# A two-layer graph attention kernel: products of layer 1 ahead of the next block's sums, its blocks in another order, and another beginning of layer 0

## The chip, the cores and the metric

The kernel runs on one core of one Trainium2 chip. The metric is the device time of one execution in microseconds (us). The core has five engines with queues of their own: TensorE (PE in the profile; its weight loads are PEld), VectorE (DVE), ScalarE (ACT), GpSimd (POOL) and SyncE (SP), and 16 DMA engines that they feed.

## What is computed

Two layers of graph attention over 2708 nodes of 1024 features, with a residual and a layer norm after each. The adjacency matrix has about 16 ones in a row.

```python
def layer0(x, adj):                       # Wf, bf, Wg, bg, W, bW
    f = x @ Wf + bf
    g = x @ Wg + bg
    e = relu(f @ g.T)
    attention = softmax(where(adj > 0, e, NEG), axis=1)
    return attention @ (x @ W + bW)

def layer1(x, adj):                       # W, a1, a2
    h = x @ W
    e = leaky_relu(h @ a1 + (h @ a2).T, 0.2)
    attention = softmax(where(adj > 0, e, NEG), axis=1)
    return relu(attention @ h)

x = layernorm(x + layer0(x, adj))
x = layernorm(x + layer1(x, adj))
```

## The kernel before

**Lists instead of a matrix.** A first stage (to about 220 us) reads the adjacency matrix, makes a list of neighbours of each node, sorts the nodes by the length of their lists and deals them out. It also multiplies `Wf` and `Wg` into one matrix `M`. After that both layers work on lists. A path for other inputs (`general_path`) is not run here.

**Blocks, groups and tiles.** The nodes stand in 22 blocks: block 0 has 20 nodes, the other 21 have 128 each, in four groups of 32. The neighbours of a group are fetched in tiles: one tile is one indirect DMA, issued by GpSimd, that brings 128 rows of 1024 numbers (four neighbours of each of 32 nodes), 0.5 MB. How many tiles a block needs is fixed by the constants `SORTED` and `BLOCKS` (lines 40 to 58): 3 for block 0, 15 for blocks 1 and 21, 16 for blocks 19 and 20, and 20 for each of the others, 405 in all. Both layers fetch all 405. Layer 0 fetches rows of `x` into a ring of 20 slots; layer 1 fetches rows of the table `T1`, which layer 0 wrote, into 32 slots (`ring` and `more`). `Layer.gathers` (line 656) issues the next gathers in order, each as soon as the tile that held its slot has been used. `SL` holds the lists, `SL0` a copy for the first tiles with its indices clamped.

**A block's work in layer 1** (lines 988 to 1110):

- `scores1` (line 1009): VectorE takes a score from a column of each tile, then `Layer.soft` (line 663) makes the weights: maxima, an exponential on ScalarE, the weights spread into matrices `st`, and row sums `rs`.
- `Layer.sums` (line 693): TensorE first adds `rs` over a group's four parts (`pt`), then adds up the tiles with their weights in the PSUM tile `po`; four groups run side by side. Each tile that is done frees its slot. ScalarE then scales `po` into `y` by the reciprocals.
- `turn` (line 517): TensorE transposes `y` into `pt` tiles, ScalarE copies them to `yT`.
- `product` (line 535): `yT` times `W1` (in the buffer `M`) in a PSUM tile `pm`: 32 matmuls in the trace. Block 0, with only 20 nodes, uses `split_product` (line 558): the eight pieces of the sum run side by side in four parts of the array, ScalarE copies the parts out, and a second product with `rep` adds them up in all four places.
- `close1` (line 1027): the residual comes by a DMA from `X1S` on SP's queue, VectorE adds and normalises (`norm`, line 594), ScalarE applies it to `z`, and GpSimd scatters `z` to the output.

Layer 0 is built in the same way, with more: the product of `x` and `M` comes first (`f_product`, line 796), is copied by ScalarE so that each group of 32 rows stands four times (`Fr`), and is multiplied by each tile on VectorE (`dots`, line 812). After the sums comes the product with `Wt` (`W`). `close` (line 828) also writes `X1S` and scatters to `T1`.

**What sets the order.** The engines' work is wrapped in `InOrder` (line 61): each engine runs its instructions strictly in the order in which the program issues them. So the order of the lines is the schedule, and an instruction that waits holds all that follow it on its engine. In layer 1 before the change, the loop over blocks (lines 1068 to 1101) issues for block k: the sums of k; the product of block k-1 (lines 1081 to 1085); the transposes of k; the closing of block k-2; the scores of k+1. The copies from `pt` to `yT` of block k follow at the start of the next round (lines 1074 to 1076). The product of k-1 thus stands between the sums of k and the transposes of k. The blocks are taken in the order 0 to 21 (line 996).

**Layer 0's beginning** (lines 858 to 906) takes block 1 first, then block 0, then 2 and on. It issues: the product of block 1 in two `pm` tiles (line 877), the copies of it to `Fr` (lines 884 to 891), q of block 2 (line 892), the product of block 0 with its copy to `Fr` (`f_small`, lines 799 to 804), the transposes of block 2 with their copies (`x_turn`, line 894), the load of block 3 and lists of 4, the product of block 2 (line 897), the load of `W` into `Wt` from ScalarE's queue (line 900), the dots of block 1 and its softmax (lines 901 to 904). Two `pm` tiles, two `pt` tiles and one `po` tile exist.

Of the kernel before, what the change touches and what calls it, by code (L numbers as in the profile page):

```python
# [8 lines left out]
F32 = mybir.dt.float32  # L9
# [3 lines left out]
ALU = mybir.AluOpType  # L13
# [93 lines left out]
def listed_path(ctx, tc, x, adj, Wf, bf, Wg, bg, W, bW, W1, a1, a2, out):  # L107

    nc = tc.nc
    P = 128  # L110
# [13 lines left out]
    Q = 4  # L124
# [430 lines left out]
            half_product(halves[h], h, n, xT, w, row)  # L555
        return halves

    def split_product(xT, w, parts, row=None):

        pm = ps_m.tile([P, H, 512], F32, name="pm")
        for h in range(H):
            c = slice(h * 512, (h + 1) * 512)
            if row is not None:
                pe.matmul(pm[:32, h, :], ones3[row:row + 3, :32], rows3[row:row + 3, c], start=True, stop=False)
            for k in range(KC // Q):
                for p in range(Q):
                    i = p * KC // Q + k
                    pe.matmul(pm[32 * p:32 * p + 32, h, :], xT[:, i, :32], w[:, i, c],  # L570
                              start=(k == 0 and (row is None or p > 0)), stop=(k + 1 == KC // Q))
        act.copy(parts, flat(pm))
        yield
        pm = ps_m.tile([P, H, 512], F32, name="pm")
        for h in range(H):
            pe.matmul(pm[:, h, :], rep, parts[:, h * 512:(h + 1) * 512], start=True, stop=True)
        return pm

    def whole(steps):

# [42 lines left out]
    def cut(most, turns, order):  # L623


        units, at = [], 0
        for i, b in enumerate(order):
            u = Unit()
            u.b, u.gs, u.at = b, groups[b], at
            u.G, u.T, u.n = len(u.gs), max(TILES[g] for g in u.gs), nrows[b]  # L630
            u.tiles = [(k, g, t) for k, g in enumerate(u.gs) for t in range(TILES[g])]
            u.col = {(k, t): m for m, (k, g, t) in enumerate(u.tiles)}
            u.tiles.sort(key=lambda m: (m[0] // turns, m[2]))
            u.sc = scores[i % 2][:, :u.G, :u.T]
            assert len(u.tiles) <= min(most, MOST)
            at += len(u.tiles)
            units.append(u)
        return units

    class Layer:  # L640
# [2 lines left out]

        def __init__(self, units, rings, width, table, stp):
            self.units, self.table, self.width, self.stp = units, table, width, stp
            self.slots = [(t, i) for t in rings for i in range(t.shape[1])]
            self.count = len(self.slots)
            self.order = [(u, g, t) for u in units for _, g, t in u.tiles]
            assert self.count <= sum(TILES[:NSL0])
            self.next, self.free, self.most = 0, set(), len(self.order)  # L650

        def rows(self, m):
# [3 lines left out]
        def gathers(self):  # L656
            while self.next < min(self.most, len(self.order)) and (self.next < self.count or self.next - self.count in self.free):
                u, g, t = self.order[self.next]
                idx = SL[:, g, t:t + 1] if self.next >= self.count else SL0[:, g, t:t + 1]
                gather(pool, self.rows(self.next), self.table, idx)  # L660
                self.next += 1

# [95 lines left out]
    with ExitStack() as s0s:  # L758
# [37 lines left out]
        def f_product(b):  # L796
            F[b] = product(nrows[b], xTs.pop(b), M, 0)

        def f_small():


            pm = whole(split_product(xTs.pop(0), M, yp.tile([P, D], F32, name="y"), 0))
            Fr[0, 0] = zs[:, :D]
            act.copy(Fr[0, 0], flat(pm))

        def replicate(b, k):

            Fr[b, k] = frp.tile([P, D], F32, name="Fr")
# [43 lines left out]

        def first_gathers(g0, g1):

            dve.tensor_scalar(SL0[:, g0:g1], SL[:, g0:g1, :], float(N - 1), None, op0=ALU.min)
            lay.gathers()

        load_x(1)
# [22 lines left out]
        for steps in (spread1, spread0):  # L881
            for _ in steps:
                pass
        for k in range(Q):
            Fr[1, k] = frp.tile([P, D], F32, name="Fr")
        for ks in ((0, 1), (2, 3)):
            for h in range(H):
                c = slice(h * 512, (h + 1) * 512)
                for k in ks:
                    for p in range(Q):  # L890
                        act.copy(Fr[1, k][32 * p:32 * p + 32, c], halves[h][32 * k:32 * k + 32, h, :])
        q_dot(2)
        f_small()
        x_turn(2)
        load_x(3)
        load_lists(4)
        f_product(2)
        spread2 = q_spread(2)
        next(spread2)
        act.dma_start(Wt, W.rearrange("(k p) d -> p k d", p=P))  # L900
        dots(units[0], 0, len(units[0].tiles))
        lay.most = len(lay.order)
        first_gathers(5, NSL0)
        soft(units[0])
        for _ in spread2:
            pass
# [81 lines left out]
    with ExitStack() as s1s:  # L988
# [4 lines left out]
        x1 = [rb, u1b]  # L993
        z1 = [u2b, zp.tile([P, D], F32, name="z1")]
        more = new_pool("ring1", 1).tile([P, R1 - R0, TW], F32, name="more")
        units = cut(R1, Q, range(NB))
        lay = Layer(units, [ring, more], TW, T1[:, :], stp)
        prod, yTs, y = {}, {}, {}


        fq = ovp.tile([P, NB, Q], F32, name="fq")
# [22 lines left out]
            dve.tensor_add(u.sc, u.sc, masked(u))  # L1024
            lay.soft(u)

        def close1(b):
            m, xt, z = valid[b], x1[b % 2], z1[b % 2]
            sp.dma_start(xt[:m], X1S[start[b]:start[b] + m, :])
            pm = prod.pop(b)  # L1030
# [5 lines left out]
            if b + 1 < NB:  # L1036
                dve.scalar_tensor_tensor(z[:m], flat(pm)[:m], 0.0, xt[:m], op0=ALU.max, op1=ALU.add)
            for _ in norm(z, m, None if b + 1 < NB else add):
                pass
            yield  # L1040
            scatter(out, ids[:m, b:b + 1], z[:m])
# [22 lines left out]
        pool.memset(over, 0.0)  # L1064
        scores1(units[0])
        closing = iter(())
        waiting = []
        for k, u in enumerate(units):
            nxt = units[k + 1] if k + 1 < len(units) else None
            b = u.b  # L1070
            back = b - 1 if b > 0 else None
            po = ps_s.tile([P, H, 512], F32, name="po")
            y[b] = yp.tile([P, D], F32, name="y1")
            if back is not None:
                for _ in yTs[back][1]:
                    pass
            if k == NB // 2 + 1:
                count_over()
            lay.sums(u, po, {6: [lambda s=closing: [None for _ in s]]}, y[b])
            closing = iter(())  # L1080
            if back is not None:
                if back > 0:
                    prod[back] = product(P, yTs.pop(back)[0], M)
                else:
                    prod[back] = whole(split_product(yTs.pop(back)[0], M, z1[1]))
            yT = tp.tile([P, KC, P], F32, name="yT")
            steps = turn(y.pop(b), nrows[b], yT, halves=True)
# [24 lines left out]

@with_exitstack
# [361 lines left out]
```

## Time and profile before

| | us |
|---|---|
| median of 3 runs | 1781.02 (1780.73 to 1785.28) |
| the profiled execution | 1778.93 |
| its span, first to last instruction | 1777.1 |
| busy: PE | 1573.1 (89%) |
| busy: DVE | 1171.4 (66%) |
| busy: ACT | 636.4 (36%) |
| busy: POOL | 1182.5 (67%) |
| layer 0, from block 1's product to the last scatter to T1 | about 228 to 1157 |
| layer 1, from its first gather to the end | 1157.4 to 1777.1 |

Times inside the execution are us from the first instruction. A line of a timeline gives the start, the duration, the engine, the operation, what it writes and reads (by the program's names), how many such instructions were merged, and in brackets how long the engine stood idle before it and what it waited for. Nearly all instructions have line 71, since one helper issues them; the names of the tiles tell them apart. In layer 1 `M` holds `W1`; in layer 0 it holds the product of `Wf` and `Wg`. The matmuls are pipelined, so that the end of one and the start of the next can overlap by some tenths.

### The profile page before, as it was taken

How to read it: one execution, taken by the hardware profiler on the slowest of the kernel's cores; microseconds unless marked ns; L12 is line 12 of the kernel's file. 1: busy time of each engine (PE TensorE's matmuls, PEld its weight loads, DVE VectorE, ACT ScalarE, POOL GpSimd, SP SyncE). 2: the span in 40 equal slices, each digit the busy share in tenths (PEclk: the TensorE clock that was granted, in tenths of full speed). 3: DMA queues.
4: the chain of work that ended last, by engine and by line, in shares of the span. 5: the costliest groups of instructions: out<-in, count | busy, mean ns of one | idle time of the engine just before them, and what ended most of it. 6: DMA issues, size and time to landing. Idle time of an engine off the chain costs nothing. (4 is left out here: it accounts for less than half of the span.)

```text
span 1777.1 us, 22911 instructions
## 1 busy us (share of the span) xinstructions
PE 1573.1 (89%) x7313; PEld 667.6 (38%) x7313; DVE 1171.4 (66%) x3539; ACT 636.4 (36%) x861; POOL 1182.5 (67%) x1191
## 2 busy tenths in 40 slices
PE   4999479899999999999999999637989988989996
PEld 2444234344444444444444444213333333333342
DVE  5879855888888888988888887513342433424442
ACT  4544454444444455555555544101111111111111
POOL 7878476467666666666666663177777777777740
PEclk9999779999999999999999999959989999999998
DMA  7646168568777777777777777299999999999960
GB/s 283 237 169 238 40 233 301 208 224 296 282 285 274 264 250 255 280 284 287 279 291 283 268 281 281 103 358 346 363 386 392 392 364 394 384 392 388 366 259 37
DMA packets 149982, 501.86 MB, mean 282 GB/s; under 512 B 32565, under 2 KB 32597, under 8 KB 147144
## 3 DMA queue, kind: packets, MB, share of 16 engines
q0 software_dynamic: 132032, 427.36, 64.8%
q1 hardware_dynamic: 10202, 55.72, 8.3%
q10 hardware_dynamic: 7618, 17.23, 2.7%
q8 instruction: 59, 0.97, 0.2%
q14 instruction: 71, 0.58, 0.1%
HBM read 509.64 MB, written 33.75 MB: 306 GB/s over the span
## 5 line engine op out<-in xcount | busy, mean ns | idle before, releaser
L71 POOL DMA_INDIRECT ring<-in_x_dram,SL x405 | 432.0, 1067 | 256.2 <-issue 89.0
L71 DVE SCALAR_TENSOR_TENSOR j<-ring,Fr 128x1024 bf16<-128x1024 f32 x402 | 494.9, 1231 | 77.0 <-DMA ring<-in_x_dram,SL 49.8
L71 ACT COPY Fr<-pm 32x1024 f32<-32x1024 f32 (+2 forms) x353 | 340.5, 965 | 20.0 <-PE pm L71 15.3
L71 PE MATMUL po<-ring,st 128*32 128x512 f32 x2660 | 338.6, 614 | 0.1
L71 POOL DMA_INDIRECT ring<-T,SL x260 | 259.6, 998 | 83.8 <-issue 58.0
L71 PE MATMUL pm<-M,xT 128*128 128x512 f32 (+1 forms) x704 | 309.7, 617 | 0.4 <-ACT xT L71 0.4
L71 PE MATMUL pm<-Wt,xT 128*128 128x512 f32 (+1 forms) x704 | 303.5, 599 | 0.0
L71 PE MATMUL pm<-M,yT 128*128 128x512 f32 (+1 forms) x704 | 298.5, 595 | 0.3 <-ACT yT L71 0.3
L71 ACT ACTIVATE scores<-scores 128x24 f32<-128x24 f32 (+5 forms) x44 | 9.8, 222 | 640.7 <-DVE scores L71 640.7
L71 PEld LDWEIGHTS pm<-M,yT 128*128 128x128 f32 (+1 forms) x704 | 127.2, 186 | 170.2 <-issue 169.7
L71 PEld LDWEIGHTS pm<-M,xT 128*128 128x128 f32 (+1 forms) x704 | 127.0, 190 | 170.6 <-issue 169.9
L71 PEld LDWEIGHTS pm<-Wt,xT 128*128 128x128 f32 (+1 forms) x704 | 125.0, 186 | 151.8 <-issue 151.4
L71 POOL DMA_INDIRECT more<-T,SL x145 | 144.1, 994 | 44.0 <-issue 32.8
L71 PEld LDWEIGHTS po<-ring,st 128*32 128x32 f32 x2660 | 102.5, 114 | 183.9 <-issue 180.0
L71 DVE TENSOR_SCALAR scores<-ring,f1q 128x2 f32<-128x2 f32 (+5 forms) x98 | 21.8, 245 | 211.3 <-DMA ring<-T,SL 209.6
L409 POOL TENSOR_TENSOR adj<-adj,iota 128x2708 f32<-128x2708 f32 (+3 forms) x23 | 130.5, 5684 | 24.9 <-ACT adj L71 24.8
L71 ACT ACTIVATE y<-po,ri 128x512 f32<-128x512 f32 (+1 forms) x88 | 55.8, 683 | 232.5 <-PE po L71 214.6
L412 DVE MAX8 cand<-adj 128x8 f32<-128x136 f32 (+2 forms) x440 | 97.2, 284 | 37.4 <-POOL adj L409 37.4
L71 PE MATMUL pm<-halfT,WfT 128*128 128x512 f32 x256 | 113.9, 600 | 1.1 <-ACT WfT L71 1.1
L71 POOL DMA_INDIRECT SL<-LD,idq x85 | 85.5, 1006 | 25.8 <-issue 20.9
L71 PE MATMUL pt<-rs,stack 128*32 128x1 f32 x680 | 14.1, 179 | 98.0 <-DVE rs L71 53.4
L71 PE MATMUL po<-more,st 128*32 128x512 f32 x580 | 94.2, 651 | 0.0
(198 smaller groups left out, 1416.9 us busy)
## 6 DMA issues: line engine op xcount, KB each, us to landing
adj<-in_adj_dram SPq DMA_DIRECT2D x21, 1354.0 KB, 5.8
X1S<-z SPq DMA_DIRECT2D x20, 512.0 KB, 6.4
ring<-in_x_dram,SL POOLq DMA_INDIRECT x405, 6.2
u1b<-X1S SPq DMA_DIRECT2D x11, 512.0 KB
rb<-X1S SPq DMA_DIRECT2D x10, 512.0 KB, 7.3
ring<-T,SL POOLq DMA_INDIRECT x260, 7.3
rows<-in_L_gnn_Wg_dram ACTq DMA_DIRECT2D x8, 512.0 KB, 4.5
rows<-in_L_gnn_Wf_dram ACTq DMA_DIRECT2D x8, 512.0 KB, 3.6
```

Of the source, the lines that this page charges most:

```text
L71: made = self.tc.keep_in_program_order(op(*args, **kwargs))
L409: nc.gpsimd.tensor_tensor(k[:n, cut], k[:n, cut], iota[:n, cut], op=ALU.mult)
L412: nc.vector.max(cand[:n, s, :], k[:n, s * SEG:min((s + 1) * SEG, N)])
```

## The change

In layer 1 the transposes of a block, their copies and its product now follow its own sums directly, ahead of the scores and sums of the next block; its closing is issued one round after its sums instead of two. The blocks are taken in the order of their tiles, fewest first: 0, 1, 21, 19, 20, 2, 3, ... 18. The buffers that alternate by block now alternate by the place in that order, and `SL0` is filled anew for the blocks whose tiles come first.

In layer 0's beginning the transposes of block 2 and the first part of block 0's product are issued right behind block 1's product. The latter goes to a `po` tile instead of a `pm` tile. The copies of block 2's transposes stand in the middle of those to `Fr` of block 1; the copy of block 0's parts stands behind them; block 0's second product and its copy to `Fr` come after block 2's product, ahead of the load of `Wt`.

```diff
-    def split_product(xT, w, parts, row=None):
+    def split_product(xT, w, parts, row=None, pm=None):
-        pm = ps_m.tile([P, H, 512], F32, name="pm")
+        pm = ps_m.tile([P, H, 512], F32, name="pm") if pm is None else pm
         for h in range(H):
...
+        yield
         act.copy(parts, flat(pm))
         yield
         pm = ps_m.tile([P, H, 512], F32, name="pm")
...
         def __init__(self, units, rings, width, table, stp):
...
+            self.first = {g: i for i, g in enumerate(g for u in units for g in u.gs)}
...
-                idx = SL[:, g, t:t + 1] if self.next >= self.count else SL0[:, g, t:t + 1]
+                idx = SL[:, g, t:t + 1] if self.next >= self.count else SL0[:, self.first[g], t:t + 1]
...
-        def f_small():
-            pm = whole(split_product(xTs.pop(0), M, yp.tile([P, D], F32, name="y"), 0))
-            Fr[0, 0] = zs[:, :D]
-            act.copy(Fr[0, 0], flat(pm))
...
+        xTs[2] = tp.tile([P, KC, P], F32, name="xT")
+        turn2 = turn(xb[2], nrows[2], xTs[2])
+        next(turn2)
+        small_f = split_product(xTs.pop(0), M, yp.tile([P, D], F32, name="y"), 0,
+                                ps_s.tile([P, H, 512], F32, name="po"))
+        next(small_f)
         for k in range(Q):
             Fr[1, k] = frp.tile([P, D], F32, name="Fr")
         for ks in ((0, 1), (2, 3)):
...
                         act.copy(Fr[1, k][32 * p:32 * p + 32, c], halves[h][32 * k:32 * k + 32, h, :])
+            for _ in turn2:
+                pass
+        next(small_f)
         q_dot(2)
-        f_small()
-        x_turn(2)
         load_x(3)
         load_lists(4)
         f_product(2)
         spread2 = q_spread(2)
         next(spread2)
+        Fr[0, 0] = zs[:, :D]
+        act.copy(Fr[0, 0], flat(whole(small_f)))
         act.dma_start(Wt, W.rearrange("(k p) d -> p k d", p=P))
         dots(units[0], 0, len(units[0].tiles))
...
-        units = cut(R1, Q, range(NB))
+        order1 = sorted(range(NB), key=lambda b: (sum(TILES[g] for g in groups[b]), b))
+        units = cut(R1, Q, order1)
         lay = Layer(units, [ring, more], TW, T1[:, :], stp)
-        prod, yTs, y = {}, {}, {}
+        done1 = {b: i for i, b in enumerate(order1)}
+        for u in units:
+            g, at = u.gs[0], lay.first[u.gs[0]]
+            if u.at < lay.count:
+                dve.tensor_scalar(SL0[:, at:at + u.G], SL[:, g:g + u.G, :], float(N - 1), None, op0=ALU.min)
...
-        def close1(b):
-            m, xt, z = valid[b], x1[b % 2], z1[b % 2]
+        def close1(b, pm):
+            m, xt, z = valid[b], x1[done1[b] % 2], z1[done1[b] % 2]
...
-        waiting = []
         for k, u in enumerate(units):
-            nxt = units[k + 1] if k + 1 < len(units) else None
             b = u.b
-            back = b - 1 if b > 0 else None
             po = ps_s.tile([P, H, 512], F32, name="po")
-            y[b] = yp.tile([P, D], F32, name="y1")
-            if back is not None:
-                for _ in yTs[back][1]:
-                    pass
-            if k == NB // 2 + 1:
-                count_over()
-            lay.sums(u, po, {6: [lambda s=closing: [None for _ in s]]}, y[b])
-            closing = iter(())
-            if back is not None:
-                if back > 0:
-                    prod[back] = product(P, yTs.pop(back)[0], M)
-                else:
-                    prod[back] = whole(split_product(yTs.pop(back)[0], M, z1[1]))
+            y = yp.tile([P, D], F32, name="y1")
+            lay.sums(u, po, {6: [lambda s=closing: [None for _ in s]]}, y)
             yT = tp.tile([P, KC, P], F32, name="yT")
-            steps = turn(y.pop(b), nrows[b], yT, halves=True)
-            next(steps)
-            yTs[b] = yT, steps
-            if waiting:
-                closing = close1(waiting.pop())
-                next(closing)
-            if back is not None:
-                waiting.append(back)
-            if nxt is not None:
-                scores1(nxt)
+            for _ in turn(y, nrows[b], yT, halves=True):
+                pass
+            if k + 1 == NB:
+                prod = two_products(P, yT, M)
+            elif b > 0:
+                prod = product(P, yT, M)
+            else:
+                prod = whole(split_product(yT, M, z1[1]))
             for i in (2 * k, 2 * k + 1):
                 if i < NB:
                     mark_over(i)
+            if k == NB // 2 + 1:
+                count_over()
+            if k + 1 < NB:
+                scores1(units[k + 1])
+            closing = close1(b, prod)
+            if k + 1 < NB:
+                next(closing)
             if k + 2 == NB:
                 unfit = nc.values_load(flag[0:1, 0:1])
         for _ in closing:
             pass
-        b = NB - 1
-        for _ in yTs[b][1]:
-            pass
-        prod[b] = two_products(P, yTs.pop(b)[0], M)
-        for b in waiting + [b]:
-            for _ in close1(b):
-                pass
```

More of the change, by code (lines that the diff above doesn't have):

```diff
@@ L648, in __init__ @@
             self.order = [(u, g, t) for u in units for _, g, t in u.tiles]
-            assert self.count <= sum(TILES[:NSL0])
+            assert all(self.first[g] < NSL0 for _, g, _ in self.order[:self.count])
             self.next, self.free, self.most = 0, set(), len(self.order)
@@ L853, in first_gathers @@
         def first_gathers(g0, g1):
-            dve.tensor_scalar(SL0[:, g0:g1], SL[:, g0:g1, :], float(N - 1), None, op0=ALU.min)
+            at = lay.first[g0]
+            dve.tensor_scalar(SL0[:, at:at + g1 - g0], SL[:, g0:g1, :], float(N - 1), None, op0=ALU.min)
             lay.gathers()
@@ L902, in listed_path @@
         lay.most = len(lay.order)
-        first_gathers(5, NSL0)
+        for g in range(5, max(g for _, g, _ in lay.order[:lay.count]) + 1, 4):
+            first_gathers(g, g + 4)
         soft(units[0])
@@ L1025, in scores1 @@
             lay.soft(u)
-        def close1(b):
-            m, xt, z = valid[b], x1[b % 2], z1[b % 2]
+        def close1(b, pm):
+            m, xt, z = valid[b], x1[done1[b] % 2], z1[done1[b] % 2]
             sp.dma_start(xt[:m], X1S[start[b]:start[b] + m, :])
-            pm = prod.pop(b)
+            last = b == order1[-1]
             def add(h):
@@ L1034, in add @@
                 dve.scalar_tensor_tensor(z[:m, c], pm[h][:m, h, :], 0.0, xt[:m, c], op0=ALU.max, op1=ALU.add)
-            if b + 1 < NB:
+            if not last:
                 dve.scalar_tensor_tensor(z[:m], flat(pm)[:m], 0.0, xt[:m], op0=ALU.max, op1=ALU.add)
-            for _ in norm(z, m, None if b + 1 < NB else add):
+            for _ in norm(z, m, add if last else None):
                 pass
```

## The prediction, made before the result was known

> **What bounds the kernel now.** I read the busy table by stretches first, to see which engine is full where, then three timelines: GpSimd and TensorE at the end of layer 1, and all engines at the start of layer 0. In the table the columns are TensorE, weight loads, VectorE, ScalarE and GpSimd busy us (with counts), granted clock, DMA share and GB/s.
>
> ```profile
> 1280.00:1340.00 60.00, 51.32 (x274) 20.49 (x273) 20.68 (x86) 7.55 (x15) 46.27 (x63) 0.91 1.01 393
> 1340.00:1400.00 60.00, 54.79 (x281) 21.77 (x280) 20.88 (x90) 7.91 (x15) 46.55 (x62) 0.91 1.01 391
> 1640.00:1700.00 60.00, 57.01 (x280) 23.34 (x279) 24.55 (x105) 8.00 (x16) 45.59 (x47) 0.97 0.98 369
> 1700.00:1760.00 60.00, 59.12 (x278) 25.11 (x277) 22.41 (x79) 9.82 (x18) 12.55 (x13) 1.00 0.35 137
> ```
>
> In layer 1 the DMA engines are full up to 1700 us; in the last 60 us they are nearly empty and TensorE is full. GpSimd shows what feeds the DMA:
>
> ```profile
> 1708.75 0.99 POOL L71 DMA_INDIRECT ring<-T,SL  x1 [0.30 <-issue]
> 1710.05 0.99 POOL L71 DMA_INDIRECT more<-T,SL  x1 [0.30 <-issue]
> 1711.34 1.01 POOL L71 DMA_INDIRECT out_dram<-z,ids  x1 [0.30 <-issue]
> ```
>
> A gather starts every 1.295 us from 1157.38 to 1710.05, with no wait for a free slot: 404 steps (523.2 us), 17 scatters of 1.31 (22.3), 7.2 of memsets and jitter. So the gather stream paces layer 1. What follows it is TensorE:
>
> ```profile
> 1725.69 0.31 PE L71 MATMUL pt<-rs,stack 128*32 128x1 f32 x16 [0.29 <-ACT yT L71]
> 1732.82 14.00 PE L71 MATMUL pm<-M,yT 128*128 128x512 f32 x32
> 1746.66 1.04 PE L71 MATMUL pt<-ident,y 128*128 128x128 f32 x8
> 1747.99 14.00 PE L71 MATMUL pm<-M,yT 128*128 128x512 f32 x32 [0.29 <-ACT yT L71]
> ```
>
> After the last sums (end 1732.9) the product of the block *before* stands ahead of the last block's own. Layer 0's beginning:
>
> ```profile
> 244.45 0.38 PE L71 MATMUL pt<-qd,rep 32*128 32x4 f32 x2
> 254.03 0.58 PE L71 MATMUL pm<-rows,ones 3*32 3x512 bf16 x1 [9.19 <-ACT Fr L71]
> 264.78 0.39 PE L71 MATMUL pm<-rows,ones 3*128 3x512 bf16 x1
> 280.13 0.31 PE L71 MATMUL pt<-rs,stack 128*32 128x1 f32 x16
> ...
> 264.01 1.01 ACT L71 COPY z<-pm 128x1024 f32<-128x1024 f32 x1 [2.07 <-PE pm L71]
> 264.89 0.39 ACTq L71 DMA_DIRECT2D Wt<-in_L_gnn_W_dram  x1
> 270.18 0.22 ACT L71 ACTIVATE scores<-scores 128x16 f32<-128x16 f32 x1 [4.18 <-DVE scores L71]
> ```
>
> TensorE stands 9.2 us until ScalarE's copies free a `pm` tile, then does the 20-node product, then block 2's. Block 1's row sums are ready on VectorE at 271.2, but its sums start at 280.1, behind block 2's product: TensorE bounds this stretch. From here on layer 0 repeats every 41 to 42 us with TensorE 39.6 us busy, so what is won here is kept.
>
> **The Trainium skill.** "TensorE: Matmul & The Clock Gate", Part 1, says that the array falls to half clock after an idle window of about 3.4 us and needs about as long busy to come back. The trace agrees: after 4.08 us idle the half product at 353.5 takes 9.48 us, not 7.13. "DMA: Bandwidth & Descriptors", section Queues, rings and completion order, says that each DMA engine goes round the queues that have work, packet by packet, which I take as half shares for two full queues. The trace allows it: the 4 MB load of M at 1079.05 with gathers from 1082.53 keeps the share at 0.94 to 1.03 until 1104, against some 15 us for the like load of Wt, from 266 to 281, with two gathers beside it.
>
> **Layer 1, steady state.** TensorE per block after the change: row sums 0.15; sums of 20 tiles 8.77 (371.61 to 380.38); then the turn, now uncovered; product 13.9. The turn from the tail's rows: ScalarE starts y 0.1 after the sums and takes 0.68 a half, four transposes 0.5, first yT copy 0.57 behind the second y half, product at +2.2. Together 25.0. Before it was 8.77+13.9+1.04+0.4 = 24.1, so TensorE pays 0.9 more. GpSimd per 20-tile block: 20 x 1.295 + 1.31 = 27.2. TensorE still has 2.2 us to spare, and the turn costs nothing there; without that cover it would be 0.9 x 17 = 15 us. With 15 or 16 tiles TensorE needs 22.9 to 23.3, GpSimd 20.7 to 22.0: TensorE bounds four blocks, 15, 15, 16, 16 tiles, now at the start.
>
> Walk: block 0's product (cold) ends near 1189, the second block's scores are ready at 1189.7 as before. Its sums and product end 1214, the third's 1237, the fourth's 1260, the fifth's 1284. The gathers of the sixth block (20 tiles) end near 1273; last gather to row sums is 6.9 + 4.0 = 10.9 us (1710.05, 1716.96, 1720.99), so 1284. TensorE has caught up just there, and from there waits for the gathers in every block.
>
> Does a slot stall GpSimd? Of a 20-tile block, gather 13 is the first that needs a tile of the block being summed. It comes 13 x 1.295 = 16.8 us after the last gather of that block; the tile is free 10.9 + 1.3 = 12.2 us after it. 4.6 us remain; later slots free every 0.43. The new order of VectorE puts `close1(k)` behind `scores1(k+1)` and ahead of the next reciprocal: close1 takes 5.9 (1704.25 to 1710.1), z 1.24, so z is out 7.2 us after the sums begin. The y scaling behind it on ScalarE is wanted at 8.8, and the scatter at position 19 of the gathers, 6 us later still: both hidden (0.5 us late for 15 tiles). The x1 loads on SP go out as soon as their buffer is free. Three small clamps of SL0 (0.2 each) precede the first gather, which waits for the last scatter to T until 1157.38: hidden. Moving `count_over` takes TensorE's 5.88 us wait at 1494 under a product, but that wait held nobody: nothing.
>
> **Layer 1, the end.** Closing one block earlier puts 3 more scatters ahead of the last gather: 20, not 17, +3.9: 1714.0. Row sums +10.9: 1724.9. TensorE came free at 1722.8, so the clock may be half: sums 8.8 to 10.4, I take 9.4 (they are 20 tiles now, 6.9 us for 15 before): 1734.3. Turn 2.2: 1736.5. From product start to the end 29.1, as now (1747.99 to 1777.1): 1765.6. **Gain 11.5**: 13.9 for the product and 4.8 for TensorE's lateness (row sums ready 1721.0, sums begun 1725.8), less 2.4 for longer sums, 0.9 for the turn and 3.9 for the scatters. If the DMA, not GpSimd, sets the pace, three scatters and three x1 loads of 0.5 MB at about 0.41 MB/us cost 7.5 and not 3.9: gain 8. With sums warm and less jitter 13.
>
> **Layer 0.** Block 2's transposes and the 20-node product run from 244.8, warm, in 1.0 + 4.4 (as 341.2 to 345.6), into `po`, which is free: done 250.3. ScalarE inserts two xT copies (1.08) among the 0.59 us Fr copies, so block 1's first `pm` is free at 254.0 + 1.1 = 255.1. TensorE has stood 4.8 us: block 2's product cold, 17.2 (352.98 to 370.19): 272.3, against 279.9 now. Then q 0.3 and the spreading product of the 20-node block 1.8: 274.4. Its copy into Fr on ScalarE ends 275.5. **Behind that copy are queued** the Wt load and the exponential of block 1, which ran at 270.2. So block 1's row sums come at 275.7 + 1.0 = 276.7, not 271.2, and the sums start 3.4 us earlier, not 5.7.
>
> Wt is issued at 275.5, 10.6 later, and asked for at 293.6 - 3.4 = 290.2. It flows from about 277 alone until the gathers start at 281.3 (1.8 MB at 0.415 MB/us), then at half share, 2.4 MB at 0.21: 292.7, with completion an estimated 293.7. TensorE waits 3.5 us, and is then at 293.7 + 16.5 + 0.3 + 15.1 + 0.4 = 326 for block 2's sums, which VectorE has ready at 326.9 - 3.4 = 323.5; now they start at 327.07. ScalarE's z at 332.7 comes at 329.9 behind the copies of block 3's product. **Gain 2.8**; bounds: 5.7 if the product of block 2 starts warm and Wt is soon there, a loss of 1 if Wt lands at 298. Gathers delayed by Wt have 9 us of slack before VectorE wants them (landing 289.0, used 298.4).
>
> **Sum.** 11.5 + 2.8 = 14.3, I say 14. The profiled execution took 1778.93, 1.83 more than its span of 1777.1; it becomes 1765. The median of the runs is 2.1 above that execution: 1767.
>
> **Rivals.**
> *A, as worked out*, 1767: 0.52.
> *B, the Wt load eats layer 0's gain.* For it: 10.6 us later, and gathers beside it. Against: VectorE, not TensorE, was last before block 2's sums (2.77 us of wait). 1781 - 11.5 = about 1770: 0.20.
> *C, the DMA sets the pace in layer 1.* For it: shares of 0.97 to 1.01. Against: the even 1.295 us steps. Gain 8 there: 1770 with layer 0's gain, 1773 without it, up to 1776 if the three scatters also find the queues full at the end: 0.13.
> *D, slower: the clock.* The turn opens a second gap in each block, 2.2 us, just after one of about 2; if both drop the clock, a product costs 2.4 more (9.48 against 7.13) and the sums 1.6: 29.0 a block, 1.8 above GpSimd's 27.2, times 16 is 29, less 14: 1796. It decides once a block passes 27.2 + 14/16 = 28.1 us. Against it: once TensorE is behind, the wait ahead of the sums vanishes and with it one drop; at one drop a block costs 27.4. 0.07.
> *E, both layers at their better bound*, 1781 - 13 - 5.7 = 1762: 0.08.
>
> **How the numbers follow.** 1767 is A's. The range from 1760 to 1776 takes in E and C. About 0.3%, 5 us, is what a measurement of this kernel can tell from no change; A, B, E and most of C are beyond it: faster 0.88; same 0.06 (the rest of C, and D at about half its price); slower 0.06.
>
> **What would show it.** GpSimd in layer 1 still without waits after 1284 and its last gather at about 1711 (1714 less layer 0's gain); one product after the last sums, not two; sums' end to product start 2.2 us; block 1's sums at about 276.7; the Wt issue at 275.5; block 2's first Wt product near 294. Wrong would be: gaps of GpSimd on TensorE in blocks of 20 tiles, half clock in the products, or Wt after 298.

## The result and the profile after

The changed kernel takes 1769.28 us (median of 14 runs, 1763.06 to 1778.59), the kernel before, measured beside it, 1782.8 (14 runs, 1777.22 to 1788.82). The ratio is 0.9924, 95% interval 0.9911 to 0.9938: 13.5 us less, between 11 and 16. The forecast was 1767, 14 less. Ratios are taken over fast runs only (those within 1.5% of the fastest of the same kernel) and are not the quotients of the medians beside them; differences in us are worked out from the ratios.

The two profiled executions differ by less, spans of 1777.1 and 1770.6, because one execution of layer 0 differs from the next by more than its new beginning is worth: over the profiles of all kernels of the next section but `fr_late` and the two built on it, whose beginning is another, the first gather of layer 1 comes at 1153.5 to 1161.5 with the new beginning and at 1157.4 to 1164.0 with the old one. So layer 1 is counted from its first gather here, and for layer 0 the timed comparison decides.

The same stretches of the table of busy times as before, of the kernel after (columns as in the prediction: TensorE, weight loads, VectorE, ScalarE, GpSimd, clock, DMA share, GB/s):

```profile
1280.00:1340.00 60.00, 57.98 (x290) 22.84 (x289) 23.06 (x101) 7.83 (x14) 46.28 (x63) 1.00 0.97 369
1340.00:1400.00 60.00, 52.09 (x275) 20.43 (x274) 22.07 (x94) 8.04 (x15) 46.28 (x63) 0.94 1.01 389
1640.00:1700.00 60.00, 53.69 (x286) 22.07 (x285) 21.39 (x92) 7.80 (x14) 45.61 (x46) 1.00 0.99 382
1700.00:1760.00 60.00, 51.35 (x280) 20.66 (x278) 23.22 (x89) 7.80 (x14) 17.93 (x18) 1.00 0.41 158
```

The picture is that of before: full DMA engines to 1700, and then TensorE nearly alone. But TensorE was 59 us busy in the last of these stretches and is 51 now: it no longer works off a backlog. The timeline of TensorE at the end shows it:

```profile
1730.84 0.30 PE L71 MATMUL pt<-rs,stack 128*32 128x1 f32 x15 [1.35 <-DVE rs L71]
...
1740.60 1.24 PE L71 MATMUL pt<-ident,y 128*128 128x128 f32 x8 [0.85 <-ACT y L71]
1741.98 14.00 PE L71 MATMUL pm<-M,yT 128*128 128x512 f32 x32
```

One product stands behind the last sums, not two, and the sums wait for VectorE's row sums (1.35 us) and not for TensorE. The turn from sums to product is 0.85 of waiting and 1.24 of transposes, in front of a product at full speed (14.00). GpSimd's timeline there:

```profile
1717.03 1.02 POOL L71 DMA_INDIRECT out_dram<-z,ids  x1 [0.30 <-issue]
1718.35 1.02 POOL L71 DMA_INDIRECT ring<-T,SL  x1 [0.30 <-issue]
...
1720.97 0.99 POOL L71 DMA_INDIRECT more<-T,SL  x1 [0.30 <-issue]
```

The last gather starts at 1720.97, 560.6 us after the first (1160.33), with 20 scatters between. Before it was 552.7 with 17. From the last gather to the end it is 49.6 us, 67.0 before. Together layer 1 went from 619.7 to 610.3. The stream of gathers also has something of which the kernel before had little:

```profile
1413.27 1.03 POOL L71 DMA_INDIRECT more<-T,SL  x1 [0.31 <-issue]
1414.61 0.99 POOL L71 DMA_INDIRECT more<-T,SL  x1 [0.31 <-issue]
1415.90 0.99 POOL L71 DMA_INDIRECT more<-T,SL  x1 [0.30 <-issue]
1418.29 0.99 POOL L71 DMA_INDIRECT more<-T,SL  x1 [1.39 <-issue]
```

"issue" with 1.39 instead of 0.30: GpSimd stands between two gathers and no engine is named for it. There are four such places, at gathers 85, 185, 286 and 387 (counted from 0), with 0.69, 1.39, 1.76 and 0.84 us, so 3.5 us above the usual 0.30. Counted in GpSimd's DMAs, gathers and scatters, from layer 1's first gather on, they are numbers 88, 194, 300 and 406: 106 apart each time. The kernel before has one, of 0.69, and it is number 406 as well. (A 0.59 at gather 35 stands in the traces of both kernels, soon after a fill of `over`, and is not counted here.)

The beginning of layer 0, first TensorE and then ScalarE:

```profile
246.59 1.92 PE L71 MATMUL po<-M,xT 128*32 128x512 f32 x16
...
255.41 0.37 PE L71 MATMUL pm<-rows,ones 3*128 3x512 bf16 x1 [4.72 <-ACT Fr L71]
255.71 8.83 PE L71 MATMUL pm<-M,xT 128*128 128x512 f32 x16
...
264.79 7.13 PE L71 MATMUL pm<-M,xT 128*128 128x512 f32 x16
...
276.01 0.30 PE L71 MATMUL pt<-rs,stack 128*32 128x1 f32 x16 [2.15 <-DVE q L71]
276.52 8.76 PE L71 MATMUL po<-ring,st 128*32 128x512 f32 x60 [0.20 <-PE pt L71]
...
292.12 4.13 PE L71 MATMUL pm<-Wt,xT 128*128 128x512 f32 x9 [0.51 <-DMA Wt<-in_L_gnn_W_dram]
...
324.73 0.39 PE L71 MATMUL pt<-rs,stack 128*32 128x1 f32 x16 [2.79 <-DVE rs L71]
```
```profile
273.90 1.01 ACT L71 COPY z<-pm 128x1024 f32<-128x1024 f32 x1 [12.76 <-PE pm L71]
273.91 0.39 ACTq L71 DMA_DIRECT2D Wt<-in_L_gnn_W_dram  x1
274.81 0.22 ACT L71 ACTIVATE scores<-scores 128x16 f32<-128x16 f32 x1
```

The 20-node product now stands in the idle stretch of before, in `po`; the rest of that stretch, 4.72 us, is still long enough for half of block 2's product to run slow (8.83 against 7.13). ScalarE waits 12.76 us for the spread product of block 0, and the `Wt` load and the exponential of block 1 stand behind its copy. Block 1's sums start 4.1 us earlier than before, the first product with `Wt` has to wait only 0.51, and block 2's sums start at 324.73 instead of 327.07.

### The profile page after: what moved, and what is told of

It reads as the page before. It is cut to its first block, busy times and chain, and to the rows that moved or that the text cites. A ratio compares the mean times of both kernels' runs of the same rounds, so it can differ in the third digit from the quotient of the medians.

```text
span 1770.6 us, 22920 instructions
## 1 busy us (share of the span) xinstructions
PE 1576.4 (89%) x7313; PEld 663.3 (37%) x7313; DVE 1169.7 (66%) x3539; ACT 641.8 (36%) x861; POOL 1190.7 (67%) x1191
## 5 line engine op out<-in xcount | busy, mean ns | idle before, releaser
L71 POOL DMA_INDIRECT ring<-in_x_dram,SL x405 | 439.4, 1085 | 251.9 <-issue 90.2
L71 PE MATMUL pm<-M,xT 128*128 128x512 f32 x672 | 305.3, 608 | 0.0
L71 PEld LDWEIGHTS pm<-M,xT 128*128 128x128 f32 x672 | 126.4, 193 | 163.0 <-issue 163.0
L71 DVE TENSOR_SCALAR scores<-ring,f1q 128x4 f32<-128x4 f32 (+4 forms) x98 | 21.7, 239 | 205.1 <-DMA ring<-T,SL 202.9
L71 ACT ACTIVATE z<-z,sh,rstd 128x1024 f32<-128x1024 f32 (+1 forms) x32 | 39.7, 1242 | 142.8 <-DVE sh L71 140.9
L71 DVE TENSOR_SCALAR scores<-more,f1q 128x3 f32<-128x3 f32 (+3 forms) x64 | 14.4, 232 | 109.7 <-DMA more<-T,SL 105.7
```

The lines of the kernel that those rows point to most:

```text
L71: made = self.tc.keep_in_program_order(op(*args, **kwargs))
```

## The experiments

The theory is the sum of the prediction: 2.8 from layer 0; in layer 1 the removed product and the order of blocks, less scatters. The rivals are that an order of blocks is worth nothing, that the DMA is the pace, that the turn costs clock.

**The two layers apart.** First only layer 0's new beginning, with layer 1 as before:

```diff
-        order1 = sorted(range(NB), key=lambda b: (sum(TILES[g] for g in groups[b]), b))
+        order1 = list(range(NB))
...
-            for _ in turn(y, nrows[b], yT, halves=True):
-                pass
...
+            steps = turn(y.pop(b), nrows[b], yT, halves=True)
+            next(steps)
```


> Only the new beginning of layer 0; layer 1 keeps its old structure and order of blocks. Theory (the prediction's: the head start of layer 0 is kept to its end): 2.8 us less than before, ratio 0.9984; block 2's sums start about 2.3 us earlier than in the kernel before (327.07), and the first gather of layer 1 is earlier than 1157.4 by the same. Rival (the head start is given back in later blocks, as the one profile after suggests, where that gather starts at 1160.3): 0 us, ratio 1.000.

Measured: 1776.18 against 1780.01, ratio 0.9983 (0.9970 to 0.9995), 3.0 us less, between 1 and 5. Its layer 1 does the same work in the same order as that of the kernel before, and took 616.2 us from the first gather to the end (552.9 to the last gather, 63.3 behind it), 3.5 less than in the profile of the kernel before: TensorE was 2.7 us late for the last sums and not 4.7. By so much can two profiles of one layer 1 differ. Then only layer 1's part, with layer 0's beginning as before:

```diff
-        xTs[2] = tp.tile([P, KC, P], F32, name="xT")
-        turn2 = turn(xb[2], nrows[2], xTs[2])
...
         q_dot(2)
+        f_small()
+        x_turn(2)
```


> Only the changes in layer 1 (product ahead and fewest tiles first); layer 0 begins as before. Theory: 11.5 us less than before, ratio 0.9935. Rival (all of the gain is layer 1's, none layer 0's): 13.5 us, ratio 0.9924. From layer 1's first gather to the end the profile should take about 610 us, as in the changed kernel, against 619.7 before.

Measured: 1772.36 against 1780.01, ratio 0.9951 (0.9934 to 0.9967), 8.7 us less, between 6 and 12, and 610.1 from first gather to end as in the whole change. Layer 0's part agrees with the prediction's 2.8. Layer 1's is 2.8 short of its 11.5 in the middle, though its interval just reaches it; the profiles, with 610 now and 616 or 620 with the old layer 1, say 6 to 10.

**The order of the blocks apart.** The whole change with the blocks in natural order:

```diff
-        order1 = sorted(range(NB), key=lambda b: (sum(TILES[g] for g in groups[b]), b))
+        order1 = list(range(NB))
```


> The whole change, but layer 1's blocks in their natural order, so that blocks of 16, 16 and 15 tiles end it. Theory: TensorE needs 23.3, 23.3 and 22.9 us for these blocks and GpSimd 22.0, 22.0 and 20.7, so that TensorE falls 6.9 us behind and starts the last sums that much after the row sums are ready; shorter sums (6.8 for 9.4) give 2.6 back: 4.3 us slower than the changed kernel, about 10 us less than before (ratio 0.9945). Rival (the order does nothing, the product ahead does all): as the changed kernel, 0.9924.

Measured: 1767.57, ratio 0.9925 (0.9907 to 0.9942), the same as the whole change. The mechanism that made me expect a loss is there all the same, in TensorE's timeline of this kernel:

```profile
1714.46 13.04 PE L71 MATMUL pm<-M,yT 128*128 128x512 f32 x30
1727.42 0.31 PE L71 MATMUL pt<-rs,stack 128*32 128x1 f32 x16
...
1735.45 1.23 PE L71 MATMUL pt<-ident,y 128*128 128x128 f32 x8 [0.83 <-ACT y L71]
1736.83 14.00 PE L71 MATMUL pm<-M,yT 128*128 128x512 f32 x32 [0.15 <-ACT yT L71]
```

The last sums follow the product of the block before without a gap: TensorE is late, 5.3 us behind the row sums, which VectorE had at 1722.1. The stretch behind the last gather is 6.0 us longer than in the whole change (55.6 and 49.6). But the stream of gathers is 6.5 shorter: 554.1 from first to last, with one scatter less (1.3) and none of the four stalls (3.5; the other 1.7 are not assigned).

The sorted order put on the kernel before, with its order of work and layer 0's old beginning:

> Layer 1 in the order of fewest tiles first with the old structure (the product of a block after the next block's sums), layer 0 as before. Theory: the last row sums are ready at the same time as before, TensorE no longer starts late (4.8 us) but sums longer (2.4 us): 2.4 us less than before, ratio 0.9987. Rival (the order does nothing): ratio 1.000. In the profile two products follow the last sums, and TensorE waits for the last row sums.

Measured: 1781.59 against 1780.01, ratio 1.0009 (0.9995 to 1.0023). Against the first kernel of this section, which has the same structure of layer 1 in natural order, it is 2.0 us shorter behind the last gather (61.3 and 63.3) and its stream 2.3 longer (555.2 with 18 scatters, 552.9 with 17). So the sorted order is worth nothing that these runs can tell, in either structure: what it wins behind the last gather it loses ahead of it. Layer 1's gain is there without it, in `natural`, so it is that of the product moved ahead, with the earlier closing that comes with it.

**The stalls.** If the x1 loads, which the same block end issues on SP's queue into full DMA engines, are behind the stalls, they go with them. This kernel leaves out the loads, and so layer 1's residual:

```diff
-            sp.dma_start(xt[:m], X1S[start[b]:start[b] + m, :])
```


> The changed kernel without the 22 loads of the residual x1 in layer 1 (0.5 MB each; the add takes what is in the buffer, so this leaves out layer 1's residual). Theory (GpSimd's issue of gathers sets the pace, 1.295 us each; the stalls of 0.4 to 1.5 us at gathers 85, 185, 286 and 387 are times in which the full DMA holds it up): these stalls vanish, the time from the first to the last gather falls from 560.6 to about 556.5 us, 4 us under the changed kernel. Rival A (the DMA sets the pace throughout): 11.5 MB at about 0.41 MB/us, up to 28 us under it. Rival B (the stalls have nothing to do with DMA load): they stay, 0 us.

Measured: 1761.39, ratio 0.9893 (0.9867 to 0.9919). Where the second stall stood, GpSimd keeps its step in this kernel's timeline:

```profile
1405.97 1.02 POOL L71 DMA_INDIRECT out_dram<-u2b,ids  x1 [0.30 <-issue]
1407.29 1.03 POOL L71 DMA_INDIRECT more<-T,SL  x1 [0.30 <-issue]
...
1409.92 0.99 POOL L71 DMA_INDIRECT more<-T,SL  x1 [0.30 <-issue]
1411.22 0.99 POOL L71 DMA_INDIRECT more<-T,SL  x1 [0.30 <-issue]
```

No stall is left in the whole stream, which takes 556.4 us with its 20 scatters: 552.7 of before plus three of 1.3 is 556.6. So the scatters cost what the prediction said, and the rest came with the loads. The loads alone do not make it: `natural` has all of them and no stall. The time is about 5.5 us under that of the whole change, though the two intervals overlap a little (0.9911 to 0.9919); in the profile the stream is 4.3 shorter and the stretch behind the last gather 2.5 (47.1 and 49.6).

The stalls come every 106 DMAs of GpSimd. To see whether that count places them, five gathers were put ahead of layer 1:

```diff
+        for t in (x1[0], x1[1], z1[0], z1[1], more[:, R1 - R0 - 1, :D]):
+            gather(pool, t, x, ids[:, 1:2])
         lay.gathers()
```


> The changed kernel with five more 128-row gathers of x ahead of layer 1's first gather, into buffers that are free there, in the 5.5 us in which GpSimd waits for the last scatter to T. GpSimd's stalls in the changed kernel come every 101 gathers, 5 or 6 DMAs behind a scatter; 100 gathers and 5 scatters are just five blocks. Theory (every 105 or so of its DMAs GpSimd has to wait if much is in flight, and in this order of blocks that always falls behind a scatter and a load of x1): five DMAs more move that point to the scatter itself, the stalls shrink, and first to last gather takes 557 us in place of 560.6; the time is 0 to 3 us under the changed kernel, since the first gather comes about 1 us later. Rival (the stalls hang on the order of the blocks alone): they stay at the same gathers, and the time is 0 to 1 us over it.

Measured: 1768.68, ratio 0.9935 (0.9911 to 0.9959); the stream takes 561.2. Three stalls are left, at gather 181, at a scatter behind gather 281 and at gather 382; with 1.17, 1.76 and 1.68 us they are together as long as the four were. Counted from layer 1's first gather they are DMAs 189, 295 and 401, each exactly five before one of the whole change, as the count says. The old structure agrees: `l0_only` has waits of 0.53 and 1.58 at DMAs 194 and 406, and `order_only` of 0.49, 0.90 and 1.03 at 194, 300 and 406 (the 0.53 and the 0.90 are put down to an engine by the profile, TensorE and VectorE). So the count of GpSimd's DMAs places the stalls, and moving them saved nothing. What decides how long a stall is, and why `natural` has none, is open.

**A slower turn.** The forecast's slower rival was that the turn's gap costs clock. ScalarE copies `y` onto itself ahead of the transposes, some 1.3 us more for each block:

```diff
+            for h in range(H if b > 0 else 0):
+                c = slice(h * 512, (h + 1) * 512)
+                act.copy(y[:, c], y[:, c])
             for _ in turn(y, nrows[b], yT, halves=True):
```


> The changed kernel, with y of every 128-node block of layer 1 copied onto itself by ScalarE before its transposes: two copies of 128x512, about 0.65 us each, so that the uncovered turn is 1.3 us longer in each of 21 blocks. Theory (while gathers set the pace TensorE has 1.3 to 2.6 us to spare in a block, as its waits for row sums in the changed profile show): 1.3 us at the end and up to 4 in the short blocks at the start, in all 2 to 6 us over the changed kernel, ratio 0.9935 to 0.996. Rival (TensorE sets the pace in layer 1, and the turn is paid in each block): 27 us over it, ratio 1.0075.

Measured: 1776.44, ratio 0.9971 (0.9953 to 0.9989), about 8.4 us more than the whole change: more than the 2 to 6 expected, far less than the rival's 27. TensorE's timeline of it:

```profile
1471.51 1.82 PE L71 MATMUL pt<-ident,y 128*128 128x128 f32 x8 [1.97 <-ACT y L71]
1473.16 14.96 PE L71 MATMUL pm<-M,yT 128*128 128x512 f32 x32
1488.04 0.31 PE L71 MATMUL pt<-rs,stack 128*32 128x1 f32 x16
```

The gap ahead of the transposes is 1.97 instead of 0.88 in blocks like this, and now the transposes take 1.82 and not 1.24, the product 14.96 and not 14.00. The granted clock agrees: 0.94 from 1400 to 1460, where the whole change has 1.00. The next row sums follow the product without a wait: from 1460.63 to 1488.04 a block takes 27.4 us, and TensorE, not GpSimd with its 27.2, sets the pace. 1.1 us of gap, 0.6 of transposes and 1.0 of product make 2.7 more in each block, and use up all that TensorE had to spare. The expectation had counted the added copies and not the slower product.

**Layer 0's copy out of the way.** ScalarE's copy of block 0 to `Fr` waits 12.76 us, with the `Wt` load and block 1's exponential behind it. Both are put ahead of it:

```diff
-        Fr[0, 0] = zs[:, :D]
-        act.copy(Fr[0, 0], flat(whole(small_f)))
+        pm_f = whole(small_f)
         act.dma_start(Wt, W.rearrange("(k p) d -> p k d", p=P))
...
         soft(units[0])
+        Fr[0, 0] = zs[:, :D]
+        act.copy(Fr[0, 0], flat(pm_f))
```


> The changed kernel, with the copy of the 20-node product into Fr moved on ScalarE's queue from ahead of the Wt load and block 1's exponential to behind them. Theory (that copy held both: the row sums of block 1 and the Wt load came 5 and 9 us late): block 1's sums start at about 274 in place of 276.0, warm (7.1 us in place of 8.8), the Wt load goes out at about 261; 2 to 4 us under the changed kernel, ratio 0.9905 to 0.9915. Rival (what is won at the start of layer 0 is given back later in it): as the changed kernel, 0.9924.

Measured: 1763.05 against 1781.3, ratio 0.9898 (0.9878 to 0.9919), 18.2 us less than before. ScalarE's timeline:

```profile
268.69 0.22 ACT L71 ACTIVATE scores<-scores 128x16 f32<-128x16 f32 x1 [9.54 <-DVE scores L71]
272.20 1.01 ACT L71 COPY z<-pm 128x1024 f32<-128x1024 f32 x1 [3.29 <-PE pm L71]
```

The exponential runs 6.1 us earlier; block 1's sums start at 272.10 behind TensorE's own work and block 2's at 319.02 instead of 324.73. By the ratios that is 4.6 us below the whole change, though the two intervals overlap a little (0.9911 to 0.9919). The expectation was 2 to 4. Of the versions that compute everything it is the fastest that was measured.

**Scatters behind the last gather, and light blocks spread.** Two kernels on top of the last: one holds two scatters back until the last gather is out, the other puts blocks 19, 20 and 21 between the heavy ones.

```diff
-            lay.sums(u, po, {6: [lambda s=closing: [None for _ in s]]}, y)
+            if k == NB - 3:
+                held, closing = closing, iter(())
+            late = [held, closing] if k == NB - 2 else [closing]
+            lay.sums(u, po, {10 if k == NB - 2 else 6: [lambda s=late: [None for c in s for _ in c]]}, y)
```


> The kernel with the Fr copy behind the Wt load and the exponential, and besides two scatters of layer 1 (of the blocks at places 18 and 19 of 22) issued behind the last gather, no longer ahead of it. Theory (GpSimd's issue sets the pace, 1.31 us a scatter): the last gather comes 2.6 us earlier (558.5 us after the first, 561.2 without), and the time falls 2.6 us, to a ratio of 0.9883. Rival (what leaves GpSimd's queue there is not on the path that sets the end): 0.9898 as without.

```diff
-        order1 = sorted(range(NB), key=lambda b: (sum(TILES[g] for g in groups[b]), b))
+        order1 = [*range(7), 19, *range(7, 11), 20, *range(11, 15), 21, *range(15, 19)]
```


> The kernel with the Fr copy behind the Wt load and the exponential, and layer 1's short blocks (16, 16 and 15 tiles) neither last nor first but spread, behind the 7th, 11th and 15th block, so that 20-tile blocks still end the layer. Theory (the stalls of GpSimd come where its point of every 100 gathers falls behind a scatter and an x1 load; sorted blocks keep it there through the layer): the short blocks move that point, first to last gather takes about 557 us in place of 561.2, the tail stays at 49.6 us as in the changed kernel: 4 us under the same kernel sorted, ratio 0.9875. Rival (20-tile blocks at the end are what makes the stalls, or TensorE falls behind in the short ones and holds slots): 561 us again, ratio 0.9898 or more.

Measured: 2191.96, ratio 1.1124 (1.1067 to 1.1181), and 2176.66, ratio 1.1041 (1.0995 to 1.1086). The kernel before took 1971.91 beside them, 190 us more than in every comparison above. So both were run again on another chip:

> The same kernel as fr_late_defer, to tell the kernel from the surroundings of its first measurement, where the kernel before itself took 1971.9 us instead of about 1782 and where the first layer-1 trace showed 20 us in each block between the last recorded matmul of the sums and ScalarE's scaling of them. If those 20 us belong to the surroundings: the kernel before near 1782 and a ratio of 0.988 (1761 us), last gather 2.6 us earlier than in fr_late counted from the first gather (558.6 instead of 561.2) because two scatters of 1.3 us lie behind it, tail no longer. If they belong to the kernel: 1.05 or more against a kernel before at 1782.

> The same kernel as spread_fr (the order of layer 1 with the light blocks 19, 20 and 21 put between the others instead of ahead of them), to tell the kernel from the surroundings of its first measurement. If the order changes nothing, as natural and order_only say: the same ratio as fr_late, 0.990 (1763 us). If spreading the light blocks takes stalls out of the gather stream without losing the scatter that sorted order wins in the tail: first to last gather 556 to 558 instead of 561.2 and a ratio of 0.9875 (1760 us). If the kernel itself is at fault in the first measurement: 1.05 or more against a kernel before at 1782.

Measured: 2183.88, ratio 1.1017 (1.0949 to 1.1084), and 2188.93, ratio 1.0892 (1.0809 to 1.0976), with the kernel before at 1987.85. The waits of the first kernel's second run (us in total, times, longest), and in a second fence ScalarE's timeline of it:

```profile
ACT y L71 <- remote: 379.6, 22, 22.8
PEld pt L71 <- ACT y L71: 346.7, 26, 22.1
```
```profile
1574.42 1.24 ACT L71 ACTIVATE z<-z,sh,rstd 128x1024 f32<-128x1024 f32 x1 [20.57 <-DVE sh L71]
1596.69 1.27 ACT L71 ACTIVATE y<-po,ri 128x512 f32<-128x512 f32 x2 [21.04 <-remote]
```

The sums of that block are out of TensorE at 1578.5 (its last matmul starts at 1577.96), and ScalarE is free from 1575.7; it begins to scale them at 1596.69, 18 us later, where in `fr_late` it is mostly 0.1. "remote" says that the event that released it is none that the profile knows. There are 22 such waits, 17 us on average and 380 in all, and TensorE waits for `y` all the while. Layer 1 takes 964 us from its first gather to the end, 610 in the runs above, and layer 0 is longer as well (first gather at 1217.6 instead of 1151.3).

What follows is limited. Neither the deferred scatters nor the spread order can be judged from these runs. Whatever delays the hand-over there hits the kernel before too (about 200 us), and these two kernels by twice that. An explanation is at hand, but only argued: before, the product of the block before stood between a block's sums and its transposes and would cover 14 us of such a delay; the change takes that cover away. No trace of the kernel before in those conditions exists, and the change alone was not run in them, so whether its own ratio would be above 1 there is open, as is the cause of the delay.

## Why the prediction was right

**Layer 1, the end: right.** From the last gather to the end 17.4 us were won against the profile of the kernel before and 13.7 against that of `l0_only`, where the steps add up to 15.4. The product is gone from behind the last sums, and TensorE's lateness with it: 0.15 us from row sums to sums. The 4.8 that the prediction gave for this lateness is what one execution had; `l0_only` had 2.7. The turn is 2.2 as said. The sums began 9.9 after the last gather, not 10.9; the sums took 8.9, not 9.4; from product start to the end it is 28.6, not 29.1.

**Layer 1, the stream: the step that was mis-sized.** "3 more scatters ... +3.9" measured +8.0 (7.3 to 8.5 if `l1_only`, `phase5` and `fr_late`, with the same layer 1, and `l0_only`, with the old one, are taken in). The scatters themselves do cost 3.9, as the kernel without x1 loads shows; of the other 4 some 3 are the stalls of GpSimd, which that kernel does not have (3.5 above its step, 0.4 in the kernel before), and the last 1 is not assigned. They are not a matter of scatters alone: in natural order the stream has two more than before, no stall, and is 1.4 longer. The prediction looked for stalls on slots only ("4.6 us remain"), rightly found none, and took even steps of 1.295 for proof that GpSimd alone sets the pace. Rival C, with the DMA as pace, put layer 1's gain at 8, and with 6 to 10 in the profiles and 8.7 timed the truth lies nearer to it than to 11.5, though in the form of a few stalls and not of a slower step.

**The order of the blocks: a wrong reason inside a right sum.** The walk over short blocks is right in kind: TensorE falls up to 5.8 us behind in the short blocks, catches up with the heavy ones and then waits for row sums (1.96 at 1428.27, 2.52 at 1455.96), and natural order leaves it 5.3 us late at the end. It caught up at 1342 and not at 1284, when it was still 3 us late; no gather was held up by that. But what sorting wins there it gives back in the stream, and the prediction priced only the winning side.

**Steady state: right, and the nearest to going wrong.** TensorE's block was worked out as 25.0 against GpSimd's 27.2, with 2.2 to spare; from 1428.27 to 1455.96 less the wait of 2.52 it is 25.2. The slower turn shows how narrow that is: two copies of 1.3 us became 2.7, through slower TensorE work, and TensorE was the bound. Rival D's mechanism is therefore real in part: a turn of 2.2 us cost no clock and one of 3.6, from the end of the sums to the product, did; where between them it begins was not measured. "TensorE: Matmul & The Clock Gate", Part 1, in the Trainium skill speaks of an idle window of about 3.4 us; here 1.97 us of idle time, with transposes after it, already made the product 1 us slower, a part of a drop and not a whole one.

**Layer 0: right in its gain, with errors that cancel.** Block 1's sums were forecast for 276.7 and began at 276.01, the `Wt` issue for 275.5 and came at 273.91. The forecast took these sums at their length of before; behind 2.15 us of waiting they took 8.76, where `fr_late`, without that wait, has 7.07, so TensorE asked for `Wt` at 291.6 and not at 290.2. `Wt` was forecast for 293.7 by half shares between two full queues, taken from what the Trainium skill says in "DMA: Bandwidth & Descriptors", section Queues, rings and completion order, and it was waited for until 292.12. The half shares are in the trace: from 286 to 290 the queue of this load moved 0.88 MB and that of the gathers 0.80. But the load was not alone ahead of that, as the forecast had it: from 277 to 281.3 it moved 1.31 MB and not 1.8, beside gathers issued before it. That its landing agrees to 1.6 us is in part luck. Its wait was 0.51, not 3.5, so rival B did not come about; and what block 2's sums waited for was VectorE (2.79), as before the change, and not TensorE as forecast. z followed 2.3 earlier than before (330.37), forecast 2.8. The timed 3.0 (1 to 5) agrees. That the exponential and `Wt` stood behind the copy of block 0 was seen and priced, and `fr_late` shows the price: some 4.6 us in the whole.

**The sum.** 8.7 and 3.0 from the halves make 11.7, and the whole gave 13.5; within the intervals these agree. The forecast was 11.5 and 2.8. That the whole came within 1 us of it owes something to luck: the stream cost 4 us more than was priced, and the parts taken singly say about 2 us less than the whole.

## What to carry to other kernels

Before an independent piece of work is moved out from between a producer and its consumer, ask what hand-over it covered and how much that hand-over may grow before the engine becomes the bound; here 1.3 us more cost 8. Where a steady stream of DMAs sets the pace beside full DMA engines, price each extra DMA at its own length, and then look for stalls beyond that: here three more scatters account for 3.9 us of a stream that grew by 8. And where a copy that nobody needs soon waits on a queue ahead of a load or an exponential that is needed, try it behind them: here that was worth some 4.6 us more.

## What the runs showed of the hardware that was not expected

- The stalls of GpSimd's gather stream all stand 106 of its DMAs apart (numbers 88, 194, 300 and 406 from layer 1's first gather), in both structures of layer 1, though not every kernel stalls at each of them; they last up to 1.8 us above its step (2.13 instead of 0.30 at gather 185 of `fr_late`). Five DMAs issued ahead move the places by exactly five, and the stalls are absent when the 22 loads of 0.5 MB on SP's queue are left out; the whole change in natural order, with those loads, has none either. What the period belongs to is open.
- On two occasions, on two chips, the kernel before ran about 200 us longer than elsewhere and two variants of the change about 400 longer than the version they were built on, these with mostly 10 to 20 us in a block of layer 1 between the last matmul of the sums and ScalarE's start (0.1 in that version), released by an event that the profile does not know. The granted clock over layer 1 was 0.79 there (1250 to 2150), where it is 0.97 otherwise (1350 to 1700 of the version they were built on); but TensorE was busy for only 548 of those 900 us, so the clock need not be the cause.
